# A convolution, Fourier and quantised feed-forward block: a new order of steps, the first image loaded ahead of the constants, and clearing on GpSimd

## The chip, the cores and the metric

The kernel runs on one core of a Trainium2 chip. The metric is the device time of one execution in microseconds (us). Before the change the median of three runs is 7464.09 us (7460.79 to 7466.0).

A core has engines with instruction queues of their own: TensorE (PE in the profile; its weight loads are PEld), VectorE (DVE), ScalarE (ACT), GpSimd (POOL) and SyncE (SP), which here only issues DMA transfers. Each queue is worked off in order, and the queues meet at semaphores.

## The reference, cut to what matters

For 64 images of 96 channels and 56x56 pixels:

```python
# layer 0
y = silu(bn(einsum('bchw,oc->bohw', x, expand_w)))       # 96 -> 192 channels
y = channel_shuffle(shift_groups(y))                     # four groups moved by one pixel
y = silu(bn(bn(depthwise3x3(y)) + bn(y * id_w)))
se = sigmoid(grouped(relu(grouped(mean(y, (2, 3))))))
x = silu(bn(einsum('bchw,oc->bohw', y * se, proj_w)) + x)
# layer 1, on t[b, n, c], n = 3136 pixels
h = relu(bn(layernorm(t) @ w1.T))
X = fft(h, axis=1); xr = relu(X.real*rd - X.imag*idg + rb); xi = relu(X.imag*rd + X.real*idg + ib)
t = t + bn(ifft(xr + 1j*xi, axis=1).real @ w2.T)
t = t + qlinear(relu(qlinear(layernorm(t), W1, b1)), W2, b2)   # operands rounded to 8 bits, sums to 16
```

## The kernel before, in words

The work on one image is cut into 56 kinds of step, and each kind has several instances: `x_in` 7 (eight image rows each), `ea_mm` 7, `i1_mm` 3, `h_mm` 21, `o_st` 7 and so on. A step is a small function (lines 376 to 912). Names that end in `_mm` issue matrix products on PE. `_ev` and its kin take a product out of PSUM, mostly on ACT (`ea_ev`, `dw_ev`, `h_ev`, `f1_ev`, `f2_u`, `i1_ev`) or on DVE (`w1_ev`, `i2_ev`, `f2_s`). `c_pow`, `n_pow` and `o_f` run on GpSimd. `x_in` and `o_st` issue two DMAs each on SP, which move an eighth-of-an-image stripe of the input or output.

The first layer of an image is `ea`/`eb` (expansion, the shift being a shifted window), `dw` (depthwise taps on PE for 128 channels) beside `lt` (nine taps on DVE for the other 64), `se` and `pj` (projection and residual). The second is `c`/`sp` (statistics), `w1`, the 56x56 Fourier transform in two factors (`f1`, `f2`), `w2`, the inverse in two factors (`i1`, `i2`), the second normalisation (`n`, `x`) and the feed-forward part (`h`, `o`).

Which step follows which is written out by hand. `PLAN` (lines 42 to 112) gives each instance a due time within an image, `PERIOD` the distance of two images; all instances of all images are sorted by due time and issued in that order (lines 921 to 928). The due times have no other use: they set the order within each queue, and by it also which buffer an instance gets, because a tile is handed out when it is issued and takes a buffer whose last reader has been issued.

```python
    with tc.manual_schedule():
        for _, b, k, i in sorted((b * PERIOD + when, b, k, i) for b in ... for k, step in ... for i, when in ...):
            STEPS[k](b, i)
```

Three images are in work at a time. There are two PSUM buffers of two banks (`psa_buf`, used by `w1`, `f1`, `f2`, `w2`, `i1`, `i2` in turn through `mix_ps`, line 356) and four of one bank (`psb`) for all else. There is one buffer `xi` for the padded input (line 166), so a stripe of the next image may be loaded once `pj_add` has read the rows that it overwrites.

Ahead of that list comes the setup (lines 166 to 354): loads of weights and tables on SP, ACT and GpSimd queues, folding of the normalisations into scales and shifts (`bn_fold`, `row_fold`), and clearing of buffers. Here the framework orders the instructions of each queue itself, and the order differs from that of the text. `row_fold` (line 260) fetches four rows of parameters to all partitions with a GpSimd DMA into a tile of two buffers (tag `ue`), takes a square root on ACT and works up the scale on DVE. It is called for the expansion, the projection, `bn1` (line 293, whose scale goes into `w1s`, line 298) and `bn2` in this order. The one product of the setup is L300, the centred `w1`; it stands first in PE's queue. The expansion's folded shift is copied into a row of `ex_w` by a DMA (line 277).

Of the kernel before, what the change touches and what calls it, by code (L numbers as in the profile page):

```python
# [7 lines left out]
F32 = mybir.dt.float32  # L8
F16 = mybir.dt.float16
F8 = mybir.dt.float8e5  # L10
AF = mybir.ActivationFunctionType
ALU = mybir.AluOpType
# [4 lines left out]
HW = 56  # L17
NPIX = HW * HW
MID = 192
HID = 384  # L20
CP = 112
TILES = ((0, 64), (64, CP))
GAP = 48
RPC = 8
NCH = HW // RPC
NT = 3
CH = RPC * HW
PAD = HW + 2
HH = HW // 2
PJ = 7  # L30
NG = 5
NK = HW // 2 + 1
NJ = HW // 2
# [8 lines left out]
PERIOD = 116.056  # L42
PLAN = {
    "x_in": (-142.751, -132.334, -138.890, -139.641, -151.208, -133.652, -137.370),
    "ea_mm": (-127.116, -124.446, -119.920, -94.498, -104.745, -112.167, -106.964),
    "ea_ev": (-125.252, -124.279, -119.721, -94.105, -94.974, -110.456, -105.960),
    "eb_mm": (-110.852, -109.364, -102.468, -94.672, -100.705),
    "eb_ev": (-109.889, -108.508, -98.175, -94.671, -100.704),
    "dw_mm": (-77.186, -75.415, -71.686, -59.708, -58.836, -58.630),
    "dw_ev": (-67.184, -68.088, -65.354, -62.005, -53.949, -53.481, -53.376, -53.432),  # L50
    "lt": (-93.236, -91.843, -90.397, -86.333, -83.176, -78.618, -75.060, -71.072, -58.358),
    "ls": (-56.957,),
    "se1_mm": (-52.674,),
    "se1_ev": (-52.590,),
    "se2_mm": (-49.560,),
    "se2_ev": (-47.764,),
    "se2_th": (-46.882,),
    "se2_pw": (-44.842,),
    "pj_mm": (-44.604, -44.263, -36.259, -33.499),
    "pj_add": (-41.623, -41.337, -40.573, -40.255, -32.468, -30.814, -32.509, -32.127),  # L60
    "pj_ev": (-41.036, -40.637, -40.429, -36.736, -30.334, -29.230, -31.146, -29.797),
    "c_mm": (-24.403, -20.404, -19.123, -17.297, -18.726, -9.644, -8.872),
    "c_sq": (-23.198, -19.663, -17.391, -16.366, -11.963, -8.651, -8.871),
    "c_v": (-21.831, -17.939, -17.390, -11.021, -10.842, -8.366, -8.657),
    "c_pow": (-19.058, -12.292, -10.931, -8.952, -1.526, -3.948, -1.526),
    "sp_v": (-8.951, -1.525),
    "sp_mm": (-6.057, 0.802),
    "sp_ev": (-5.461, 1.113),
    "w1_mm": (1.423, -2.619, 3.588, 18.203, 8.943, 12.171, 13.999, 16.535),
    "w1_ev": (3.273, -0.045, 7.600, 20.920, 11.591, 14.999, 15.957, 19.212),  # L70
    "f1_mm": (21.608, 26.248, 24.638, 31.810, 32.559, 32.004),
    "f1_ev": (25.169, 25.895, 30.841, 28.844, 27.556, 26.595, 32.009, 32.411, 36.910, 36.732, 36.699, 35.929),
    "f2_mm": (37.220, 36.994, 44.528, 54.196, 60.721, 63.959),
    "f2_u": (39.991, 41.910, 38.664, 38.665, 56.185, 56.316, 56.071, 58.643, 62.858, 62.962, 66.464, 67.055),
    "f2_s": (42.369, 43.646, 41.684, 42.524, 58.496, 59.412, 59.011, 59.603, 66.349, 66.780, 67.365, 69.133),
    "f2_r": (44.699, 46.227, 59.499, 60.966, 71.228, 72.985),
    "f2_p": (46.153, 47.154, 60.124, 60.967, 72.402, 74.345),
    "w2_mm": (70.359, 71.061, 73.352, 79.154),
    "w2_ev": (70.421, 73.788, 79.483, 82.773),
    "i1_mm": (82.811, 83.639, 91.924),  # L80
    "i1_ev": (86.931, 93.317, 99.344),
    "i2_mm": (102.107, 101.737, 110.644, 111.766),
    "i2_ev": (106.004, 107.037, 104.651, 104.395, 113.248, 110.645, 115.503, 113.393),
    "n_mm": (109.042, 108.523, 116.336, 120.505, 126.604, 126.539, 137.374),
    "n_sq": (109.105, 109.021, 116.337, 120.506, 127.174, 126.540, 137.375),
    "n_v": (109.642, 109.022, 116.338, 120.507, 127.975, 126.902, 138.122),
    "n_pow": (110.809, 110.170, 116.496, 122.658, 132.126, 129.135, 139.318),
    "n_x": (112.520, 110.693, 119.248, 123.053, 133.298, 130.929, 139.362),
    "x_mm": (113.125, 114.113, 121.321, 126.216, 135.244, 138.382, 142.002),
    "x_ev": (114.896, 115.709, 126.025, 126.217, 137.926, 142.365, 142.302),  # L90
    "h_mm": (
        144.408, 144.539, 142.955, 151.653, 146.123, 151.741, 165.593, 167.081, 167.021, 179.037, 181.701, 184.163,
        183.315, 191.401, 194.122, 202.572, 203.025, 214.978, 205.482, 214.132, 209.133,
    ),
    "h_ev": (
        146.457, 147.163, 146.728, 153.132, 153.156, 154.262, 168.465, 171.753, 169.119, 180.037, 185.733, 184.280,
        187.040, 192.972, 195.243, 203.531, 205.107, 216.376, 208.878, 222.205, 212.052,
    ),
    "h_b": (
        146.899, 148.834, 148.614, 154.505, 157.941, 159.836, 170.515, 176.287, 174.097, 185.812, 187.639, 185.918,  # L100
        191.781, 195.030, 198.861, 204.123, 206.545, 220.428, 209.152, 226.370, 218.475,
    ),
    "h_q": (
        149.384, 151.139, 150.029, 159.215, 163.340, 163.159, 172.257, 183.329, 182.397, 187.024, 188.763, 189.403,
        196.328, 198.478, 200.406, 208.755, 210.002, 221.499, 217.314, 229.791, 224.579,
    ),
    "o_mm": (153.028, 179.101, 192.712, 203.850, 207.474, 223.800, 230.382),
    "o_ev": (154.015, 179.621, 193.552, 207.958, 209.955, 223.824, 232.254),
    "o_b": (167.276, 193.254, 201.506, 209.696, 210.604, 235.187, 237.499),
    "o_f": (171.766, 199.519, 206.356, 219.602, 231.322, 259.139, 253.186),  # L110
    "o_st": (197.792, 218.616, 214.282, 229.895, 257.122, 313.688, 263.438),
# [4 lines left out]
def conv_attn_ffn(  # L116
# [38 lines left out]
    nc = tc.nc  # L155
    NB = x.shape[0]

    const = ctx.enter_context(tc.tile_pool(name="const", bufs=1))
# [10 lines left out]
    nc.sync.dma_start(out=xi[GAP : GAP + 1].rearrange("p a b -> p (a b)"), in_=tab_ones)  # L169

    def load_x(b, i):

        rows = slice(i * RPC, (i + 1) * RPC)
        for p0, c0 in ((0, 0), (64, 48)):
            nc.sync.dma_start(
                out=xi[p0 : p0 + 48, 1 + i * RPC : 1 + (i + 1) * RPC, 1 : HW + 1],
                in_=x[b, c0 : c0 + 48, :].rearrange("c (a b) -> c a b", b=HW)[:, rows, :],
            )


    def load(ap, shape, name, eng=nc.sync, dtype=F32):
        t = const.tile(shape, dtype, name=name)
        eng.dma_start(out=t, in_=ap)
        return t

    ex_w = load(expand_t, [CP, MID], "ex_w")
    mid = load(mid_par, [128, 2, 22], "mid")
    mid_g = load(mid_grp, [128, NG, 12], "mid_g")
# [19 lines left out]
    l_tab = load(tab_l, [128, NK, CP], "l_tab", nc.scalar)  # L208
    inv_tab = load(tab_inv, [CP, 2, HW], "inv_tab", nc.scalar)
    r_tab = load(tab_r, [128, HW, HW], "r_tab", nc.scalar)  # L210

    eps = const.tile([128, 1], F32, name="eps")
    nc.vector.memset(eps, 1e-5)
    mhalf = const.tile([128, NJ], F32, name="mhalf")
    nc.vector.memset(mhalf, -0.5)
# [35 lines left out]
    eyes = load(tab_eyes, [128, 32], "eyes")  # L251
# [7 lines left out]

    def row_fold(src, n, rows, name):  # L260

        b = work.tile([128, 4, n], F32, tag="ue", name=name + "_p")
        nc.gpsimd.dma_start(out=b[0:rows], in_=src.rearrange("(o f) c -> o f c", o=1).to_broadcast([rows, 4, n]))
        s = work.tile([128, 2, n], F32, tag="s", name=name)
        s = s[0:rows]
        nc.scalar.activation(s[:, 0], b[0:rows, 3, :], AF.Sqrt, bias=eps[0:rows])
        nc.vector.reciprocal(s[:, 0], s[:, 0])
        nc.vector.tensor_tensor(s[:, 0], s[:, 0], b[0:rows, 0, :], ALU.mult)
        nc.vector.tensor_tensor(s[:, 1], b[0:rows, 2, :], s[:, 0], ALU.mult)
        nc.vector.tensor_tensor(s[:, 1], b[0:rows, 1, :], s[:, 1], ALU.subtract)  # L270
        return s

    s = row_fold(expand_row, MID, CP, "ex_row")
    nc.vector.tensor_tensor(ex_w, ex_w, s[:, 0], ALU.mult)
    nc.sync.dma_start(out=ex_w[GAP : GAP + 1, :], in_=s[0:1, 1, :])
    ex_b = const.tile([CP, 2, 2, 2, 16], F32, name="ex_b")
    nc.vector.memset(ex_b, 0.0)
    for e in range(2):  # L280
        nc.vector.tensor_copy(
            ex_b[:, e, :, e, :], ex_w[:, 128:MID].rearrange("p (u e i) -> p u e i", u=2, e=2)[:, :, e, :]
        )
# [43 lines left out]

    e_a = const.tile([128, PAD, PAD], F32, name="e_a")  # L330
    nc.gpsimd.memset(e_a, 0.0)
    e_b = const.tile([128, HH + 2, PAD], F32, name="e_b")
    nc.gpsimd.memset(e_b, 0.0)
    for i in range(NT):
        nc.vector.memset(t_buf[i], 0.0)

    buf_h = const.tile([128, C * HW + 8], F32, name="buf_h")
    nc.vector.memset(buf_h, 0.0)
# [6 lines left out]
    nc.vector.memset(buf_g, 0.0)  # L345
# [30 lines left out]
    def x_in(b, i):  # L376
        load_x(b, i)
# [726 lines left out]
```

## Time and profile before

| | |
|---|---|
| median of three runs | 7464.09 us |
| the profiled execution: its time | 7463.64 us |
| its span, first to last instruction | 7461.9 us |
| PE / PEld / DVE / ACT / POOL busy | 7176.9 / 5259.2 / 4829.5 / 4654.4 / 1513.6 us |
| PE idle in all | 285.0 us |
| first matrix product (L300) | at 43.30 us |
| last matrix product | 7453.65 us |
| PE busy from 300 to 7300 us | 6822.69 of 7000 us |

A wait in the profile is the idle time of an engine just before an instruction, put down to what released it. "issue" means that nothing which the profile records was waited for. Lines such as L786 are lines of the kernel before; `psa`, `ps_c` and so on are the tiles that are written.

PE's order in one period, from the sort (the number in brackets is the image, relative to the one whose `dw` it starts with; adjacent instances of one kind are put together):

```
before
dw0 dw1 dw2[0] f2_2[-1] h6 h8 h7[-2] f2_3[-1] dw3 dw4 dw5[0] f2_4[-1] h9[-2] o1[-2] se1[0] f2_5[-1] h10[-2] se2[0]
h12 h11[-2] w2_0 w2_1[-1] pj0 pj1[0] w2_2[-1] h13 o2 h14[-2] w2_3[-1] pj2 pj3[0] i1_0 i1_1[-1] h15 h16 o3 h18 o4[-2]
c0[0] i1_2[-1] h20[-2] c1 c2 c4[0] h19[-2] c3[0] h17[-2] i2_1 i2_0[-1] ea0[1] c5 c6[0] ea1[1] o5[-2] n1 n0[-1] sp0[0] ...
after
dw0 dw1 dw2[0] f2_2[-1] h6 h8[-2] f2_3[-1] dw3 dw4 dw5[0] f2_4[-1] h7[-2] f2_5[-1] h9[-2] o1[-2] se1[0] h10 h12 h11[-2]
se2[0] w2_0 w2_1[-1] pj0 pj1[0] w2_2[-1] h13 h14 o2[-2] w2_3[-1] pj2 pj3[0] i1_0[-1] o3 h16 h15[-2] i1_1[-1] o4 h18[-2]
i1_2[-1] h20[-2] c0 c1 c2 c4[0] h19 h17[-2] i2_0 i2_1[-1] ea0[1] c3 c5 c6[0] ea1[1] o5[-2] n1[-1] sp0[0] n0[-1] ...
```

ACT's order around the second half of `dw`: before `dw_ev4 dw_ev5 dw_ev7 dw_ev6 f2_u8 f2_u9 se1_ev`, after `dw_ev7 dw_ev6 f2_u8 h_ev7 f2_u9 dw_ev5 dw_ev4 h_ev9 o_ev1 se1_ev`. SP's order from the projection on: before `x_in4, o_st, o_st, x_in0` amid the `pj_add`, then `x_in3 x_in2 x_in6 o_st x_in5 x_in1 o_st`; after `x_in0` amid the `pj_add`, one `o_st`, and behind the last `pj_add` `x_in6 x_in2 x_in1 x_in5 x_in4 o_st o_st x_in3`.

### The profile page before, as it was taken

To read this page: it belongs to the slowest core of one execution; us is meant where nothing else is said; L and a number is where in the kernel's file an instruction comes from. 1 tells how busy PE (TensorE), PEld (TensorE's weight loads), DVE (VectorE), ACT (ScalarE), POOL (GpSimd) and SP (SyncE) were. 2 spreads that over 40 slices of the span, in tenths; PEclk is the share of its full clock that TensorE was granted. 3 is DMA by queue.
4 is the path that set the end of the run, shared out by engine and by line. 5 is a ranking of instruction groups with operands and counts; after the bars stand their busy time and mean duration, and the time that the engine had idled before them with its cause. 6 is when DMAs were issued, how large, how long until landed. Compare 5 with 4: busy or idle time off the path is not lost.

```text
span 7461.9 us, 383252 instructions
## 1 busy us (share of the span) xinstructions
PE 7176.9 (96%) x177666; PEld 5259.2 (70%) x177666; DVE 4829.5 (65%) x8795; ACT 4654.4 (62%) x9806; POOL 1513.6 (20%) x1360
## 2 busy tenths in 40 slices
PE   7999999999999999999999999999999999999997
PEld 4777777777777776777777777777777777777775
DVE  5666666666666666666666666666666666666664
ACT  3566666666665666656656666666566566665665
POOL 0221212212212122122121221221212212212112
PEclk9999999999999999999999999999999999999998
DMA  1010110110101101101011011010110110101100
GB/s 48 20 27 18 29 27 19 29 24 21 28 17 29 27 19 28 24 22 28 17 29 27 19 28 25 22 28 18 29 27 19 29 26 20 29 21 26 28 20 21
DMA packets 424331, 185.32 MB, mean 25 GB/s; under 512 B 378785, under 2 KB 422041, under 8 KB 422473
## 3 DMA queue, kind: packets, MB, share of 16 engines
q1 hardware_dynamic: 420970, 155.82, 9.1%
q8 instruction: 1392, 22.81, 1.3%
q10 hardware_dynamic: 1264, 3.48, 0.1%
q14 instruction: 209, 1.71, 0.1%
q0 software_dynamic: 496, 1.50, 0.1%
HBM read 82.80 MB, written 77.07 MB: 21 GB/s over the span
## 4 chain that ended last, share of the span: by engine, by line
PE 85%; ACT 6%; DVE 6%; issue 3%; DMA 0%; POOL 0%; POOLq 0%; SPq 0%; ACTq 0%
PE psa L653 9%; PE psa L626 9%; PE ps_d L446 8%; PE ps_eb L400 5%; PE ps_ea L383 5%; PE psa L808 5%; PE ps_pj L532 5%; PE ps_c L557 5%; PE psa L745 5%; PE ps_n L557 5%; PE psa L786 5%; PE psa L680 4%; PE ps_h L865 4%; PE ps_o L887 3%; DVE s L721 3%
## 5 line engine op out<-in xcount | busy, mean ns | idle before, releaser
L903 POOL TENSOR_TENSOR o<-t,o 112x448 f32<-112x448 f32 x448 | 613.9, 1370 | 3694.7 <-DMA out_dram<-o 1710.0
L446 PE MATMUL ps_d<-e_a,diag 32*32 32x392 f32 x36864 | 1033.2, 498 | 0.7 <-ACT d L456 0.7
L468 DVE SCALAR_TENSOR_TENSOR d_last<-e_b,taps,d_last 128x1568 f32<-128x1568 f32 x512 | 971.5, 1898 | 7.1
L875 DVE TENSOR_SCALAR y<-y,qb 128x448 f16<-128x448 f16 x1344 | 479.8, 365 | 683.9 <-ACT y L870 676.7
L568 DVE TENSOR_REDUCE v<-sq 112x4 f32<-112x384 f32 x896 | 491.3, 548 | 662.7 <-ACT sq L564 662.1
L446 PEld LDWEIGHTS ps_d<-e_a,diag 32*32 32x32 f32 x36864 | 673.6, 103 | 288.9 <-issue 40.0
L870 ACT CAST y<-ps_h 128x448 f16<-128x448 f32 x1344 | 697.2, 540 | 213.1 <-PE ps_h L865 209.5
L837 POOL TENSOR_TENSOR rs<-v,mhalf 112x4 f32<-112x4 f32 x448 | 490.3, 1099 | 1453.9 <-DVE v L569 1453.9
L881 ACT CAST h<-y 128x448 fp8e5<-128x448 f16 x1344 | 739.0, 571 | 3.0 <-DVE y L875 3.0
L653 PEld LDWEIGHTS psa<-f_tab,buf_h 128*56 128x56 f32 x24576 | 655.4, 131 | 77.8 <-DVE v L569 42.5
L626 PEld LDWEIGHTS psa<-w1c,t 112*64 112x64 f32 x14336 | 604.0, 137 | 141.4 <-DVE v L569 45.4
L653 PE MATMUL psa<-f_tab,buf_h 128*56 128x58 f32 x24576 | 688.9, 216 | 0.0
L626 PE MATMUL psa<-w1c,t 112*64 112x96 f32 x14336 | 676.2, 249 | 2.9 <-DMA t<-dev_t 1.4
L586 POOL TENSOR_TENSOR rs<-v,mhalf 112x4 f32<-112x4 f32 x448 | 447.6, 1012 | 763.6 <-DVE v L569 763.5
L638 DVE SCALAR_TENSOR_TENSOR buf_h<-psa,rs_full 128x768 f32<-128x768 f32 (+1 forms) x512 | 435.4, 851 | 137.4 <-PE psa L626 129.5
L543 DVE TENSOR_TENSOR ps_pj<-ps_pj,x 112x392 f32<-112x392 f32 x512 | 260.6, 566 | 404.5 <-PE ps_pj L537 392.3
L728 ACT ACTIVATE s<-s 128x896 f32<-128x896 f32 (+2 forms) x384 | 334.4, 887 | 288.8 <-DVE s L721 288.8
L388 ACT ACTIVATE e_a<-ps_ea 128x448 f32<-128x448 f32 x448 | 244.9, 547 | 412.5 <-PE ps_ea L383 412.5
L564 ACT ACTIVATE sq<-ps_n 112x384 f32<-112x384 f32 x448 | 214.1, 495 | 436.1 <-PE ps_n L557 434.8
L734 DVE SCALAR_TENSOR_TENSOR buf_h<-ue,s 128x448 f32<-128x448 f32 (+2 forms) x768 | 406.8, 580 | 109.4 <-ACT s L728 109.4
L549 ACT ACTIVATE t<-ps_pj,pjbn_b 112x392 f32<-112x392 f32 x512 | 281.4, 620 | 284.5 <-DVE ps_pj L543 284.5
L786 PE MATMUL psa<-inv_tab,buf_g 112*32 112x56 f32 x24576 | 350.5, 214 | 110.5 <-issue 108.8
(175 smaller groups left out, 13024.5 us busy)
## 6 DMA issues: line engine op xcount, KB each, us to landing
x<-in_x SPq DMA_DIRECT2D x896, 84.0 KB, 3.2
out_dram<-o SPq DMA_DIRECT2D x896, 84.0 KB, 2.2
l_tab<-in_tab_l ACTq DMA_DIRECT2D x1, 1624.0 KB
r_tab<-in_tab_r ACTq DMA_DIRECT2D x1, 1568.0 KB
t<-dev_t SPq DMA_DIRECT2D x64, 7.0 KB, 2.1
t<-dev_t SPq DMA_DIRECT2D x64, 5.2 KB
ex_row_p<-in_expand_row POOLq DMA_DIRECT2D x1, 336.0 KB, 4.5
s_p<-in_bn POOLq DMA_DIRECT2D x1, 288.0 KB, 3.8
```

What stands on the lines that cost most here:

```text
L446: nc.tensor.matmul(pss[r][j * 32 : j * 32 + 32], lhsT=diag[pr, tap, :], rhs=e_a[pr, r0 : r0 + PJ, dx : dx + HW], start=tap == 0, stop=tap ...
L468: nc.vector.scalar_tensor_tensor(d_last, win, w, d_last, ALU.mult, ALU.add)
L557: nc.tensor.matmul(cen[c0:c1, k, 0:C], lhsT=t_of(b)[:, n0 + c0 : n0 + c1], rhs=center, start=True, stop=True)
L568: nc.vector.tensor_reduce(v, sq, AX.X, ALU.add)
L626: nc.tensor.matmul(ps[hc * 64 : hc * 64 + 64, k, 0:C], lhsT=t[:, n0 : n0 + 64], rhs=w1c[:, hc * C : hc * C + C], start=True, stop=True,)
L653: nc.tensor.matmul(ps[r * 64 : r * 64 + HW, k, 0 : 2 * NK], lhsT=buf_h[:, n0 : n0 + HW], rhs=f_tab[:, r, :], start=True, stop=True,)
L786: nc.tensor.matmul(ps[p0 : p0 + 32, k, 0:HW], lhsT=u_v[:, oh * 48 + o, :], rhs=inv_tab[:, r, :], start=True, stop=True,)
L837: nc.gpsimd.tensor_tensor(rs, held.pop(("nv", b, g)), mhalf[0:CP, 0:4], ALU.pow)
L870: nc.scalar.copy(y16, held.pop(("h", b, i)))
L875: nc.vector.tensor_scalar(y16, y16, qb1[:, i % 3 : i % 3 + 1], 0.0, ALU.add, ALU.max)
L881: nc.scalar.copy(held["h8", b, j][:, m, :], held.pop(("y", b, i)), saturate=False)
L903: nc.gpsimd.tensor_tensor(o32, rows, o16, ALU.add)
```

## The change

It has three parts.

1. `PERIOD` and all due times of `PLAN` are replaced. The kinds of step, their number and what each does stay as they are; the order in every queue is new.
2. In the setup the load of the expansion weights is followed at once by the row of ones, the 14 DMAs of the first image (taken out of the sorted list by `if b > 0`) and the fold of the expansion with its `ex_b`. `mid`, `mid_g` and `eyes` go to ACT's queue; the two big tables `l_tab` (1624 KB) and `r_tab` (1568 KB) leave ACT's queue and come last of the loads, on SP. The copy of the folded shift goes from SP to GpSimd.
3. The clearing of the three `t_buf`, `buf_h` and `buf_g` goes from DVE to GpSimd, and that of `e_a` and `e_b`, on GpSimd already, moves up in the text.

The diff, with the rows of the plan that the prediction speaks of:

```diff
-PERIOD = 116.056
+PERIOD = 116.1319138
...
-    "x_in": (-142.751, -132.334, -138.890, -139.641, -151.208, -133.652, -137.370),
+    "x_in": (-152.0645309, -141.2993712, -141.6679729, -127.3567477, -140.4175705, -140.8791946, -144.4420607),
...
-    "dw_ev": (-67.184, -68.088, -65.354, -62.005, -53.949, -53.481, -53.376, -53.432),
+    "dw_ev": (-77.0167479, -77.0167407, -77.0167341, -77.0167381, -60.0783737, -60.0901315, -61.6632225, -61.9014126),
...
-    "i1_mm": (82.811, 83.639, 91.924),
+    "i1_mm": (80.9444124, 84.7640673, 88.5170591),
...
-    "o_mm": (153.028, 179.101, 192.712, 203.850, 207.474, 223.800, 230.382),
+    "o_mm": (144.4008021, 172.4113645, 192.8051961, 197.2106880, 201.6982825, 222.7674293, 226.6091401),
...
     nc.vector.memset(xi, 0.0)
-    nc.sync.dma_start(out=xi[GAP : GAP + 1].rearrange("p a b -> p (a b)"), in_=tab_ones)
...
     ex_w = load(expand_t, [CP, MID], "ex_w")
-    mid = load(mid_par, [128, 2, 22], "mid")
-    mid_g = load(mid_grp, [128, NG, 12], "mid_g")
+
+    nc.sync.dma_start(out=xi[GAP : GAP + 1].rearrange("p a b -> p (a b)"), in_=tab_ones)
+    for i in range(NCH):
+        load_x(0, i)
+    eps = const.tile([128, 1], F32, name="eps")
+    nc.vector.memset(eps, 1e-5)
...
+    s = row_fold(expand_row, MID, CP, "ex_row")
+    nc.vector.tensor_tensor(ex_w, ex_w, s[:, 0], ALU.mult)
+    nc.gpsimd.dma_start(out=ex_w[GAP : GAP + 1, :], in_=s[0:1, 1, :])
...
+    e_a = const.tile([128, PAD, PAD], F32, name="e_a")
+    nc.gpsimd.memset(e_a, 0.0)
+    e_b = const.tile([128, HH + 2, PAD], F32, name="e_b")
+    nc.gpsimd.memset(e_b, 0.0)
+
+    mid = load(mid_par, [128, 2, 22], "mid", nc.scalar)
+    mid_g = load(mid_grp, [128, NG, 12], "mid_g", nc.scalar)
+    eyes = load(tab_eyes, [128, 32], "eyes", nc.scalar)
...
-    l_tab = load(tab_l, [128, NK, CP], "l_tab", nc.scalar)
     inv_tab = load(tab_inv, [CP, 2, HW], "inv_tab", nc.scalar)
-    r_tab = load(tab_r, [128, HW, HW], "r_tab", nc.scalar)
...
-    nc.sync.dma_start(out=ex_w[GAP : GAP + 1, :], in_=s[0:1, 1, :])
...
+    l_tab = load(tab_l, [128, NK, CP], "l_tab")
+    r_tab = load(tab_r, [128, HW, HW], "r_tab")
...
     for i in range(NT):
-        nc.vector.memset(t_buf[i], 0.0)
+        nc.gpsimd.memset(t_buf[i], 0.0)
...
-    nc.vector.memset(buf_h, 0.0)
+    nc.gpsimd.memset(buf_h, 0.0)
...
-    nc.vector.memset(buf_g, 0.0)
+    nc.gpsimd.memset(buf_g, 0.0)
...
     def x_in(b, i):
-        load_x(b, i)
+        if b > 0:
+            load_x(b, i)
```

## The prediction

> **What bounds the kernel now.** The page comes first. PE is busy for nearly the whole span and no other engine comes near it:
>
> ```profile
> PE 7176.9 (96%) x177666; PEld 5259.2 (70%) x177666; DVE 4829.5 (65%) x8795; ACT 4654.4 (62%) x9806; POOL 1513.6 (20%) x1360
> ...
> PE   7999999999999999999999999999999999999997
> ```
>
> The change takes no matrix product away. What it can gain lies in PE's 285.0 us of idle time (7461.9 - 7176.9), of which 43.3 us come before the first product. So the second view is the waits, asked for PE alone, with sum, number and longest:
>
> ```profile
> PE psa L786 <- issue: 108.8, 68, 2.2
> PE psa L745 <- DVE ue L724: 50.8, 64, 1.7
> PE ps_w1c L300 <- DVE w1s L298: 43.3, 1, 43.3
> PE ps_c L557 <- issue: 18.6, 20, 1.9
> ```
>
> Two waits come in every one of the 64 images: about 1.7 us in `i1_mm` (L786) for nothing recorded, and 0.8 us in `w2_mm` (L745) for `f2_s`. With the 18.6 us in `c_mm`, "issue" costs 127.4/64 = 2.0 us an image. The third view is PE's timeline of one image amid the run, to see where these fall:
>
> ```profile
> 3028.02 0.61 PE L478 MATMUL ps_se<-sums,rd_w 128*24 128x1 f32 x18
> ...
> 3031.92 1.53 PE L745 MATMUL psa<-w2a,buf_h 128*64 128x96 f32 x32 [0.83 <-DVE ue L724]
> ...
> 3050.09 2.86 PE L786 MATMUL psa<-inv_tab,buf_g 112*32 112x56 f32 x216
> 3055.03 1.00 PE L786 MATMUL psa<-inv_tab,buf_g 112*32 112x56 f32 x40 [2.08 <-issue]
> ...
> 3059.89 1.78 PE L786 MATMUL psa<-inv_tab,buf_g 112*32 112x56 f32 x128
> ```
>
> The third `i1_mm`, standing alone, runs its 128 products (and 128 loads) in 1.78 us without a break; the first two, standing together, stop after 216 of 256. No semaphore does that. The page's queue table names a suspect:
>
> ```profile
> q8 instruction: 1392, 22.81, 1.3%
> ```
>
> 22.81 MB in 1392 packets is 16.4 KB a packet, and 2 x 177666 instructions over 1392 packets is 255 a packet: PE's instructions arrive in blocks of about 256. One `i1_mm` uses up a block in 1.7 us, faster than any other step (`dw`: 576 instructions in 7.95 us). I read the wait as the next block being late: a block needs about 1.7 + 1.75 = 3.5 us to come. SP's timeline shows the six DMAs of `x_in` starting at 3050.79, so these blocks travel beside image data.
>
> [...] I go with the row, which recurs in each image where two `i1_mm` adjoin and not where one stands alone.
>
> **Steady part, step by step.**
> (a) *`i1`.* The new order puts `o3 h16 h15` between the first two (rows: 0.66 + 0.55 = 1.2 us) and `o4 h18` (0.67 + 0.28 = 0.95 us) before the third. Every block of 256 in this stretch (3 x 256 + 18 instructions) now holds one such gap: 1.7 + 1.2 = 2.9 us or 1.7 + 0.95 = 2.65 us instead of 1.7. Against 3.5 us two boundaries wait 0.6 and 0.85, and a third, half in `c_mm`, perhaps 0.1: 1.55 instead of 2.0. Besides, `x_in6` and its followers now start only behind the last `pj_add`, some 2.1 us into the stretch (the four take 1.99 us), so the first block may come sooner. I take -0.5 us an image. Ends: -1.4 (every block but one in time), and +1.2, if the unbroken run of `x_in` makes a block take 4.1 us: then the two wait 1.2 and 1.45 and the third 0.5, 3.2 in all.
> (b) *`w2`.* From the start of `f2_4` to that of `w2_0` the old order takes 3031.92 - 3025.66 = 6.26 us, 0.83 of it waiting. In the new one `h7` (0.2 us) moves in here, and `se1` comes to lean on `dw_ev4`, now last: from the start of `f2_4`, ACT does `dw_ev7`, `dw_ev6` (to 1.3), waits for `f2_4` (1.56), then `f2_u8`, `h_ev7`, `f2_u9` (0.6 + 0.45 + 0.6) and `dw_ev5`, `dw_ev4` (2 x 0.565), to 4.4 us. PE arrives at 1.5 + 0.3 + 1.1 + 0.3 + 0.66 = 3.85 and waits 0.6. With `se1`, three `h` and `se2` (0.54 + 0.67 + 0.65) `w2_0` starts at 6.3, and its `f2_s9` (3.25 + 4 x 0.65 = 5.85) is done: this wait goes, the one at `se1` comes. Behind `se1` stand the `h` products and `se2`, whose followers `se2_pw` and `pj0` have over 1 us to spare. Net 0; ends -0.3 and +0.4.
> (c) *The rest of the period.* I walked the queues in the same way. The spare times are small but not negative: `pj0` for `h_ev12` 0.35 us, `x0` for `n_x0` 0.45, `f1_4` for `f1_ev2` 0.6, `f2_1` for `f1_ev11` 0.3. Adjoining `h` products fall into 11 groups instead of 13, worth 0.1 each at most. Zero; ends -0.2 and +0.3.
> Sum: -0.5 us an image, over 63 images -32 us.
>
> **Start.** Here PE is held by L300, first in its queue:
>
> ```profile
> 4.07 2.92 POOL L331 MEMSET e_a<- 128x3364 f32 x1
> ...
> 22.49 4.54 DVE L338 MEMSET buf_h<- 128x5384 f32 x1 [1.06 <-issue]
> ...
> 33.33 0.53 POOL L263 DMA_DIRECT2D s_p<-in_bn  x1 [10.98 <-DVE ex_row L270]
> ...
> 43.30 0.98 PE L300 MATMUL ps_w1c<-w1s,gcen 96*112 96x192 f32 x2 [43.30 <-DVE w1s L298]
> ```
>
> The parameters of `bn1` are fetched at 33.33 because their buffer waits for the expansion's fold (L270), which sits in DVE behind three memsets of 2.68, one of 4.54 and loads of later constants. With the fold early and these memsets gone, its parameters (landing 4.5 us after 1.28) give a square root by about 7 and L270 by about 10. Fetch, square root and scale then take 3.87 + 0.46 + 1.34 + 3 x 0.35 = 6.7 us, so L300 could start at 17.3 and `ea` 0.9 later, at 18.2 instead of 44.20: 26 us gained. But the memsets, and now the shift's copy too, share GpSimd's queue with this fetch. At the rate of the `e_a` row (2.92/3364 = 0.87 ns a column) they take 3 x 2.73 + 4.67 + 4.83 = 17.7 us; all ahead of the fetch, behind `e_b` (8.5), it goes out at 26.8, and `ea` starts at 34.5: 9.7 us gained. Which it is depends on how the framework sorts the setup; I take the middle, -18 us. The cover for the memsets is that `t_buf` is first written at 88 us and `buf_h` at 111.
>
> The 14 DMAs of `x` (11 took 8.56 us to issue) go out from the end of the `xi` memset (4.4) and are done by some 17 us; if SP serves the two tables first (3.2 MB; the first 20 us ran at 271 GB/s, so 12 us), they end near 29, still within the span above. `mid`, `mid_g` and `eyes` add three issues of 0.45 us to ACT's queue, ahead of the square roots; the two tables that leave it gave back 0.8. `diag`, which needs `mid` and some 30 small DVE operations (26.96 to 31.96 now), is wanted 12.8 us after `ea`, when `dw` begins; DVE, free of 17.3 us of memsets, has that time. `l_tab` is needed at 141 us and `r_tab` at 200. Uncovered, a late `diag` would hold `dw` for what it is late; I put nothing.
>
> **The end.** The last 55 us (7407 to 7462) are a chain of normalisation and feed-forward steps of one image; its order changes little: 0, +-4.
>
> Sum against the profiled execution: 7463.64 - 32 - 18 = 7413.6, and the median of the runs is 0.45 above it: 7414 us.
>
> **Rivals.**
> (B) *The fetch of blocks gains nothing* (three dense blocks near each other wait as long as two did), and only the start moves: 7464 - 18 = 7446, between 7437 and 7455. For it: the stretch still holds 768 instructions in some 8 us. Against it: no two `i1_mm` adjoin.
> (C) *Slower: the blocks meet the transfers.* Place: the boundaries in `i1_1` and `i1_2`. Five stripes of `x_in` and two of `o_st` now follow each other without a break there. At 4.1 us a block the price is 3.2 - 2.0 = 1.2 us an image, 7464 + 76 - 18 = 7522. It decides from 0.52 us an image on ((18 + 15)/63), that is from about 3.75 us a block. For it: the longest wait before is 2.2 us, 3.9 a block. Against it: that was under the old burst, which began earlier.
> (D) *More than thought*: blocks in time but one and an early start: 7464 - 63 x 1.4 - 26 = 7350.
>
> **How the numbers follow.** Forecast (A) 0.55, own range 7385 to 7448; B 0.22; C 0.13; D 0.10. A measurement of this kernel can tell about 0.2% (15 us) from no change: below 7449 is faster, above 7479 slower. A lies below with 0.54, D with 0.10, B with 0.13 of its 0.22: 0.77 faster. C is 0.13 slower. 0.10 is left for the same. The range takes A, B, half of D and the beginning of C: 7368 to 7475.
>
> **What would show it.** Right: `ea` (L383) starts between 18 and 34 us; L786 shows several short waits on "issue" an image, under 1.6 us together, none of 2; L745's wait on L724 is gone and L478 waits for L456 instead. Wrong: the sum of waits on "issue" at or above 127 us (B, C); a new wait in each image on DVE, ACT or POOL that (c) has not; PE busy time off 7177 by more than 20 us.

## The result, and the profile after

The kernel after the change takes 7414.07 us (median of four runs, 7406.62 to 7424.39), the kernel before beside it 7464.03 us: a ratio of 0.9939 [0.9925, 0.9953], 50 us faster. The profiled execution has a span of 7414.7 us, 47.2 below that of before. Measured again later beside other kernels it took 7423.54 against 7467.66 us, 0.9946 [0.9932, 0.9959], 44 us. So two sets of the same comparison differ by 6 us, and smaller differences are read from traces here, not from medians.

Line numbers have moved: L809 is `i1` (it was L786), L580 `c` and `n` (L557), L768 `w2` (L745), L501 `se1` (L478), L747 `f2_s` (L724), L479 `dw_ev` (L456), L324 the first product (L300), L406 `ea` (L383). First the engine line of the page after:

```profile
PE 7188.3 (97%) x177666; PEld 5229.7 (71%) x177666; DVE 4842.3 (65%) x8790; ACT 4641.4 (63%) x9806; POOL 1589.9 (21%) x1366
```

PE's idle time is 7414.7 - 7188.3 = 226.4 us, 58.6 less than before; its busy time is 11.4 us longer. The waits of PE, after (sum, number, longest):

```profile
PE psa L809 <- issue: 97.5, 112, 2.0
PE ps_w1c L324 <- DVE w1s L322: 26.2, 1, 26.2
PE ps_c L580 <- issue: 24.5, 23, 2.9
PE ps_se L501 <- ACT d L479: 16.4, 65, 1.3
...
PE psa L768 <- DVE ue L747: 1.6, 2, 1.4
```

Three things are to be seen. The wait ahead of `w2` is gone (50.8 to 1.6 us) and one at `se1` has come (16.4). The first product starts 17.1 us earlier. But the waits on "issue" have hardly moved: 108.8 + 18.6 = 127.4 before, 122.0 now. PE's timeline of one `i1` stretch after shows why:

```profile
3031.22 1.78 PE L809 MATMUL psa<-inv_tab,buf_g 112*32 112x56 f32 x128
3032.93 0.77 PE L910 MATMUL ps_o<-h,q 128*112 128x448 fp8e5 x3
3033.54 0.54 PE L888 MATMUL ps_h<-xq,q 96*128 96x448 fp8e5 x2
3034.01 1.39 PE L809 MATMUL psa<-inv_tab,buf_g 112*32 112x56 f32 x96
3035.75 0.60 PE L809 MATMUL psa<-inv_tab,buf_g 112*32 112x56 f32 x32 [0.35 <-issue]
3036.28 0.78 PE L910 MATMUL ps_o<-h,q 128*112 128x448 fp8e5 x3
3036.89 0.35 PE L888 MATMUL ps_h<-xq,q 96*128 96x448 fp8e5 x1
3037.18 1.37 PE L809 MATMUL psa<-inv_tab,buf_g 112*32 112x56 f32 x92
3039.79 0.69 PE L809 MATMUL psa<-inv_tab,buf_g 112*32 112x56 f32 x36 [1.23 <-issue]
```

The one long pause of 2.08 us has become two shorter ones. Counted through the whole trace, every distance of over 0.7 us between two neighbouring starts of one line's loads and products (83 before, 94 after, between 300 and 7200 us) falls at the same remainder of PE's instruction count divided by 256: they are block boundaries, as the prediction read them. Summed over all boundaries between 300 and 7200 us, what these distances have beyond the usual cost 149.5 us before and 145.6 after, 0.06 us an image less.

The spans add up as follows. `dw` of the first image starts 17.3 us earlier (56.98 to 39.69). From there to `dw` of the fourth image the new order takes 6.6 us longer (311.4 to 318.0). After the `dw` of the last image it takes 4.2 less (209.7 to 205.5 us to the last product). What is left of the 47.2, some 32 us, is the period, which falls from 114.65 to 114.07 us (mean over images 3 to 60).

### The profile page after: what moved, and what is told of

Same layout as the page of the kernel before. It is cut to its first block, busy times and chain, and to the rows that moved or that the text cites. A ratio compares the mean times of both kernels' runs of the same rounds, so it can differ in the third digit from the quotient of the medians.

```text
span 7414.7 us, 383547 instructions
## 1 busy us (share of the span) xinstructions
PE 7188.3 (97%) x177666; PEld 5229.7 (71%) x177666; DVE 4842.3 (65%) x8790; ACT 4641.4 (63%) x9806; POOL 1589.9 (21%) x1366
## 4 chain that ended last, share of the span: by engine, by line
PE 93%; ACT 3%; issue 3%; DVE 1%; POOL 0%; DMA 0%; POOLq 0%; ACTq 0%; SPq 0%
PE ps_d L469 14%; PE psa L676 9%; PE psa L649 9%; PE ps_ea L406 5%; PE ps_eb L423 5%; PE psa L831 5%; PE ps_n L580 5%; PE ps_pj L555 5%; PE psa L768 5%; PE psa L809 4%; PE ps_c L580 4%; PE psa L703 4%; PE ps_h L888 4%; PE ps_o L910 3%; PE psa L713 3%
## 5 line engine op out<-in xcount | busy, mean ns | idle before, releaser
L926 POOL TENSOR_TENSOR o<-t,o 112x448 f32<-112x448 f32 x448 | 659.1, 1471 | 3629.9 <-DVE o L920 2280.0
L688 ACT COPY buf_g<-psa 128x464 f32<-128x464 f32 x768 | 388.8, 551 | 186.4 <-PE psa L676 184.7
L809 PE MATMUL psa<-inv_tab,buf_g 112*32 112x56 f32 x24576 | 373.3, 214 | 99.3 <-issue 97.5
L809 PEld LDWEIGHTS psa<-inv_tab,buf_g 112*32 112x32 f32 x24576 | 327.5, 110 | 197.5 <-issue 196.3
L866 DVE TENSOR_TENSOR xt<-ps_n,rs 112x384 fp8e5<-112x384 f32 x448 | 243.7, 556 | 315.8 <-POOL rs L860 311.4
```

Source lines behind the costliest of these rows:

```text
L809: nc.tensor.matmul(ps[p0 : p0 + 32, k, 0:HW], lhsT=u_v[:, oh * 48 + o, :], rhs=inv_tab[:, r, :], start=True, stop=True,)
L926: nc.gpsimd.tensor_tensor(o32, rows, o16, ALU.add)
```

## The experiments

**The two halves of the change.** `setup_only` has the new setup with the old plan, `plan_only` the new plan with the old setup (both keep everything else).

> The new setup with the old period and due times. If the parts simply add: the first matrix product at about 26 us instead of 43.3, and all of these 17 us kept to the end, 7447. If the new order is what loses 6.9 us of the start in the first two images (first dw to fourth dw: 311.9 us before, 318.9 after), this run keeps 311.9 and ends at 7447; if the new setup itself loses them (a table or a buffer that comes late), it shows 319 and ends at 7454.

> The new period and due times with the old setup; the first image is then loaded from the setup's queue position as before. If the parts add: first product at 43.3 us, and 7464 minus 30, 7434. The prediction's steady term alone would give 7432. If the gain of the new order needs the new start, it ends near 7464.

Measured: `setup_only` 7445.21 us, 0.9979 [0.9972, 0.9986]; `plan_only` 7438.44 us, 0.9966 [0.9958, 0.9974]; before 7463.55. The parts give 18.3 + 25.1 = 43.4 us, the whole 44 to 50: they add, within the 6 us by which two sets differ. The first product starts at 26.2 us in the one and at 43.2 in the other. The 6.6 us lost in the first images belong to the new order: from the first `dw` to the second `setup_only` needs 87.05 us, as before (87.10), `plan_only` 92.6, as after (92.4). The period is 114.66 with the old plan and 114.14 with the new.

**Step (a) undone.** `i1_together` puts the first two `i1_mm` back to back:

```diff
-    "i1_mm": (80.9444124, 84.7640673, 88.5170591),
+    "i1_mm": (80.9444124, 80.9454124, 88.5170591),
```

> The changed kernel with one due time moved, so that the second i1_mm follows the first at once and o3 h16 h15 come behind it. The prediction's step (a): two blocks in a row again, 0.5 us an image more waiting, 7414 + 32 = 7446. The rival (blocks under the unbroken run of x_in take about 4 us, so that splitting and not splitting wait alike, as the sums of the two traces say: 149.5 us before, 145.6 after): 7414, within 10 us, with waits of 2 us again in i1_mm and fewer of them.

Measured: 7421.45 us, 0.9953 [0.9937, 0.9968], and these waits:

```profile
PE psa L809 <- issue: 105.4, 102, 2.2
...
PE ps_c L580 <- issue: 22.6, 24, 2.9
```

128.0 us instead of 122.0 (118.4 in the second trace of after). The parting of the `i1_mm` is worth some 6 to 10 us of waits in all, not 32, and the time is where the rival had it. Step (a) falls.

**Do the blocks meet the image transfers?** `no_x` leaves out the loads of images 1 to 63, seven stripes each (`NB` is the number of images, 64):

```diff
-        if b > 0:
+        if b > NB:
             load_x(b, i)
```

> after without the loads of the image stripes of images 1 to 63: all images are computed from the pixels of the first, as they stand in the buffer; everything else is as in after. Theory that PE's instruction blocks are late because they travel beside the image transfers: the waits on issue in i1 and c (97.5 + 24.5 us) fall below 60 us, and the time by as much, to about 7350. Rival that a block takes 3.0 us and more whoever else transfers: the waits stay at 105 us or more and the time within 20 us of 7414.

Measured: 7395.02 us in one run, and

```profile
PE psa L809 <- issue: 82.7, 111, 1.7
...
PE ps_c L580 <- issue: 20.2, 22, 2.9
```

102.9 us, 19 less than after, and the time of this one run is 19 us less too. So the meeting that rival (C) was built on exists, but it makes about one sixth of the waits; the rest comes whether images are loaded or not. Neither expectation had the figure; the second was nearly right.

**Step (b), and where the clock comes in.** In the waits of after, `se1` waits for `dw_ev4`. `dw_ev5_early` puts ACT's `f2_u9` and `dw_ev5` further forward, to take that wait away:

```diff
-    "dw_ev": (..., -60.0783737, -60.0901315, -61.6632225, -61.9014126),
+    "dw_ev": (..., -60.0783737, -61.6500000, -61.6632225, -61.9014126),
...
-        56.0332668, 59.7855946, 59.8827469,
+        54.8412044, 59.7855946, 59.8827469,
```

> The changed kernel with dw_ev5 put ahead of f2_u8 and f2_u9 ahead of h_ev7 on ScalarE. By the walk of step (b): se1 can start 0.4 us earlier (dw_ev4 is done at 4.05 instead of 4.4 us behind the start of f2_4), and w2_0 is still not held by f2_s9: 0.4 us an image less, 7414 - 25 = 7389. If the wait only moves on to w2_0 or se2, no change.

Measured: 7457.24 us (median of twelve, 7445.96 to 7465.32; the profiled one is the longest), 0.9996 [0.9987, 1.0004], 43 us slower than after. The wait at `se1` did go; a smaller one at `w2` came back:

```profile
PE psa L768 <- DVE ue L747: 28.3, 65, 1.6
...
PE psa L768 <- DVE gate L529: 5.9, 37, 0.2
```

28.3 + 5.9 - 16.4 - 1.6 = 16 us of waits do not make 43. PE's timeline of that kernel shows the rest:

```profile
3135.15 0.76 PE L501 MATMUL ps_se<-sums,rd_w 128*24 128x1 f32 x18
3135.84 0.86 PE L888 MATMUL ps_h<-xq,q 96*128 96x448 fp8e5 x3
3136.63 0.43 PE L516 MATMUL ps_se<-red,ep_w 24*32 24x1 f32 x32
3136.99 0.28 PE L524 MATMUL ps_se<-red,ep_w 24*64 24x1 f32 x4
3137.68 2.65 PE L768 MATMUL psa<-w2a,buf_h 128*64 128x96 f32 x32 [0.42 <-DVE ue L747]
```

The 32 products of `w2` take 2.65 us, where they take 1.53 in other images. The same kernel asked by stretches (start:end, length, busy us and count of PE, PEld, DVE, ACT and POOL, granted TensorE clock, DMA share, GB/s):

```profile
3131.10:3134.50 3.40, 3.40 (x62) 2.56 (x52) 1.68 (x4) 3.00 (x9) 0.00 (x0) 1.00 0.02 5
3134.50:3137.90 3.40, 2.98 (x66) 1.81 (x66) 2.93 (x7) 3.40 (x10) 0.00 (x0) 1.00 0.00 0
3137.90:3141.30 3.40, 3.40 (x60) 3.18 (x60) 3.05 (x8) 2.66 (x7) 1.31 (x1) 0.50 0.00 0
3141.30:3144.70 3.40, 3.40 (x92) 2.77 (x88) 1.69 (x5) 2.42 (x6) 0.00 (x0) 1.00 0.02 5
```

For one stretch of 3.41 us PE is granted half its clock. The trace notes each change of the clock: such stretches begin only at multiples of 3.413 us from one another, within 0.01 us over the whole run (all 24 in the trace of before and all 16 in that of after as well), so they are windows of a grid. In the window before this one PE waits 0.42 us and issues products of one column (L501, L516, L524) for another 1.3. The kernel before has the same thing elsewhere. Its stretches around the 2.08 us pause that the prediction showed:

```profile
3048.50:3051.90 3.40, 3.40 (x159) 2.45 (x159) 1.71 (x4) 1.10 (x3) 0.00 (x0) 1.00 0.07 15
3051.90:3055.30 3.40, 1.32 (x108) 1.20 (x100) 0.52 (x2) 1.79 (x4) 1.31 (x1) 0.99 0.64 130
3055.30:3058.70 3.40, 3.40 (x43) 2.03 (x32) 0.67 (x2) 1.56 (x4) 0.00 (x0) 0.50 0.58 131
```

Busy for 1.32 of 3.40 us, and the next window runs at half speed. Between 300 and 7200 us these windows sum to 54.6 us before, 23.9 after and 102.4 in `dw_ev5_early`; half of the 78.5 us between the last two is 39 us, and with the 16 us of waits that is 55, against 43 between the medians and 49 between the two profiled spans. In `dw_ev5_early` they come at 3137.9, 3254.0, 3370.0 and 3486.1 us: 116.05 us apart, which is 34 windows (34 x 3.413). An image that is hit becomes so long that the next one meets the grid at the same place.

**Taking the wait away.** DVE stood idle for 2.12 us ahead of `f2_s8`, held by `h_b7`, which waited for ACT. `h7_late` is `dw_ev5_early` with `h_b7` behind `f2_s9`:

```diff
-        ..., 152.3035773, 164.4059572, 171.8564611,
+        ..., 152.3035773, 164.4059572, 176.2000000,
```

> This is dw_ev5_early with one more due time moved: the DVE half of h7 (h_b7, 171.86 to 176.2) goes behind f2_s9 instead of ahead of f2_s8, where DVE stood idle for 2.12 us waiting for ACT's h_ev7. w2_0 should then find f2_s9 done. Clock theory (a PE window of 3.41 us with 1.6 us or more of idle and single-column products is followed by one at half speed; in dw_ev5_early the 0.42 us wait at w2 brings the stretch se1 to w2 to 1.75 us): without the wait the stretch has 1.35, the half-speed windows at w2 vanish (25 in dw_ev5_early, 3 in after), and the time falls by the wait and by half of some 85 us of half-speed windows: 7457 - 28 - 42 = 7387, between 7380 and 7400, faster than after by 15 to 30. Rival (the loss of dw_ev5_early is the wait at w2 and what comes after it, the clock has no part): 7457 - 28 = 7429, between 7420 and 7440. Second rival (the wait moves to another place): within 7414 to 7460, with a new wait of 0.3 us or more in each image.

Measured: 7402.33 us (7399.5 to 7410.45), 0.9917 [0.9901, 0.9934]. Half-speed windows fall from 102.4 to 10.2 us between 300 and 7200 us, and none is left at `w2`, where `dw_ev5_early` had 25. The time falls by 55 us where the waits at `w2` fell by 19 (28.3 + 5.9 to 13.6 + 1.8): the clock theory's side, 2 us outside its range. Half of the 92 us of half-speed windows and the 19 us of waits make 65, against 62 between the two profiled spans. The miss has a name in this kernel's timeline:

```profile
3119.29 0.63 DVE L744 SCALAR_TENSOR_TENSOR s<-psa,fb,ue 128x392 f32<-128x392 f32 x1 [1.70 <-ACT ue L728]
...
3124.36 0.15 DVE L529 TENSOR_TENSOR gate<-ps_se,ep_b 128x5 f32<-128x5 f32 x1
3124.59 1.53 PE L768 MATMUL psa<-w2a,buf_h 128*64 128x96 f32 x32 [0.22 <-DVE gate L529]
```

`f2_s8` now waits only for its own operand, but the second `w2` waits 0.22 us in 62 images (13.6 us) for DVE, which does `h_b9` and `o_b1` ahead of `f2_s10`. `h9_late` moves these behind the gate as well:

```diff
     "h_b": (
...
-        162.0938148, 176.2691390, 188.9411972, ...
+        162.0938148, 181.6000000, 188.9411972, ...
...
     "h_q": (
...
-        168.8971320, 181.6666748, 191.8993395, ...
+        168.8971320, 182.6000000, 191.8993395, ...
...
-    "o_b": (158.1581711, 179.3239824,
+    "o_b": (158.1581711, 181.6100000,
```

> This is h7_late with three more steps moved behind what the projection waits for: h_b9 and o_b1 on DVE from ahead of f2_s10 to behind se2_ev, h_q9 on ACT behind se2_th. In h7_late, w2_1 waited 0.22 us in 62 images (13.6 us) for DVE, which had done these two first (0.33 us each). Theory that the wait simply goes: 7402 - 13 = 7389, between 7383 and 7396, with no wait at w2 left. Rival that PE finds another wait in its place (h_q9 later on ACT, o2 later): 7398 to 7406, with a new wait of about 0.2 us in each image.

> The kernel after the change, unaltered, beside h9_late and clear_dve. By its runs so far: 7407 to 7424, median 7414; with half-speed PE windows from 300 to 7200 us of 15 to 45 us in all, as many as the time is longer by half of them.

Measured side by side: `h9_late` 7386.23 us (7382.75 to 7390.35), 0.9891 [0.9878, 0.9905]; after 7423.54 us (7421.79 to 7432.35), 0.9946 [0.9932, 0.9959]. The waits at `w2` are gone and no new one came. `h9_late` beats both kernels: 81 us below before and 37 below after. Of the 37, 64 x 0.36 = 23 lie between the last `dw` product and `w2` (6.60 us an image after, 6.23 here; 13 of them are the recorded waits at `se1`, 16.4 to 3.0), and the clock gives (118.9 - 91.1)/2 = 14, counted over the whole run. The two profiled executions of after differ in the same way, with nothing changed: spans of 7414.7 and 7420.0 us, half-speed windows of 23.9 and 34.1 us between 300 and 7200 us. Half of the difference is 5.1, the spans differ by 5.3.

**Is it single-column work, and not only idling, that lowers the clock?** `se1_twice` and its control `h_twice` issue products of `h9_late` a second time:

```diff
 se1_twice, in se1_mm
-        for i in range(9):
+        for _ in range(2):
+            for i in range(9):
 h_twice, in h_mm
-        nc.tensor.matmul(ps, ...)
+        for _ in range(2 if i in (10, 12) else 1):
+            nc.tensor.matmul(ps, ...)
```

> This is h9_late with the 18 products of se1 issued twice (the second pass overwrites the first with the same sums): 0.69 us more of single-column products an image, and no wait. Clock theory (single-column products count as idle for the clock, and a 3.41 us window with some 1.6 us of both is followed by one at half speed): from the first se1 product to w2 the stretch is then 2.75 us long and has 2.02 us of single-column work; of the positions of a fixed window 1.5/3.41 = 0.44 catch 1.6 us or more of it, so at least 28 of 64 images have a half-speed window at w2, at about 1.5 us each: 7386 + 44 + 42 = 7472 and up to 7526 if all images have one. Rival (only waits count, not single-column products, since PE is busy): 7386 + 44 = 7430, between 7424 and 7438, and no half-speed window at w2.

> The control of se1_twice: h9_late with the products h10 and h12, which stand between se1 and se2, issued twice (same result): two more products of 448 columns, 0.57 us an image, in the same place. Both theories: 7386 + 36 = 7422, between 7414 and 7430, and no half-speed window at w2, since nothing sparse is added. If half-speed windows come here too, it is the longer distance from dense work to dense work and not the single columns that counts.

Measured: `se1_twice` 7417.33 us, 0.9920 [0.9904, 0.9937]; `h_twice` 7395.97 us, 0.9894 [0.9879, 0.9909]. Both sizes were wrong: the second pass costs 0.33 us an image, not 0.69 (from `se1` to `w2` 2.06 to 2.39 us), since the row of 0.76 us contained a wait between products (in the trace of after they start 0.025 to 0.046 us apart and once 0.37 us, 0.21 of it recorded as idle); the two `h` cost 0.26, not 0.57. Both times lie below the ranges of both theories, and so do not decide between them. The sparse work of that stretch rose to some 1.7 us only, not 2.02. The direction holds, though at least 28 half-speed windows were expected: at `w2` there are 5 with `se1_twice` and none in `h9_late` or `h_twice`; in all, 30.7 us against 13.7 and 3.4. Stretches of `se1_twice` around one of the five:

```profile
2778.90:2782.30 3.40, 3.40 (x85) 2.35 (x85) 2.72 (x6) 3.31 (x10) 0.00 (x0) 1.00 0.00 0
2782.30:2785.70 3.40, 3.40 (x56) 3.18 (x58) 3.33 (x9) 2.84 (x7) 0.76 (x1) 0.51 0.02 5
```

PE counts as busy for all of the first stretch, and the second runs at half speed. So recorded idle time is not needed. But a row of `se1` contains a short wait that in part counts as busy: whether the single columns or this wait lower the clock, the two runs cannot tell. Five windows are few; the control has none. Against `h9_late` the profiled span is 33.7 us longer (7417.5 to 7383.8): 64 x 0.33 = 21 and, over the whole run, half of 118.0 - 91.1, 13.

**The start.** `clear_only` is before with the five memsets on GpSimd; `clear_dve` is after with them back on DVE.

> before with the clearing of the three t_buf, of buf_h and of buf_g on GpSimd, and nothing else. Theory that the memsets on DVE are what holds the expansion's fold (L270) and so bn1's fetch: the first product starts at 26 to 32 instead of 43.3 us. Rival that the clearing only changes the queue in which it stands ahead of the fetch (GpSimd issues it): the first product starts at 38 us or later. Time: 7464 less what the first product gains, to within 6 us.

> after with the clearing of the three t_buf, of buf_h and of buf_g back on DVE: part 3 undone, the new order of the setup kept. Theory that the loads and the fold in their new place bring the early start and the clearing has little part: the first product starts at 20 to 28 us (26.2 in after). Rival that DVE's 17 us of clearing holds the fold again: the first product starts at 34 us or later. Time: 7414 and what the first product moves, to within 8 us.

`clear_only`: first product at 42.9 us, 7474.4 us in one run against 7465.45 (9 us longer where at most 6 were expected, but inside the scatter of before, whose runs went from 7443 to 7479). Part 3 alone brings nothing; the rival holds. `clear_dve`: first product at 22.0 us, 4.2 earlier than after, and yet 7435.25 us in one run, 12 more than after beside it, where 4 less was expected. Its timeline:

```profile
6.51 0.17 DVE L260 TENSOR_SCALAR fa<-fa 128x2 f32<-128x2 f32 x1 [1.95 <-DMA fa<-in_freq_a]
...
13.33 0.52 POOL L216 DMA_DIRECT2D s_p<-in_bn  x1
...
14.28 0.29 DVE L291 TENSOR_SCALAR taps<-mid,dwbn_s,mgbn_s 128x9 f32<-128x9 f32 x1
...
38.91 4.70 DVE L367 MEMSET buf_g<- 128x5568 f32 x1 [1.11 <-issue]
...
64.19 0.48 PE L501 MATMUL ps_se<-sums,rd_w 128*24 128x1 f32 x8 [8.30 <-ACT d L479]
```

and that of after:

```profile
6.04 5.15 DVE L260 TENSOR_SCALAR fa<-fa 128x2 f32<-128x2 f32 x1 [1.48 <-DMA fa<-in_freq_a]
...
8.43 2.74 POOL L357 MEMSET t<- 112x3144 f32 x1
...
16.34 0.51 POOL L230 DMA_DIRECT2D ex_w<-ex_row  x1 [5.17 <-DVE dwbn_b L275]
...
16.88 0.52 POOL L216 DMA_DIRECT2D s_p<-in_bn  x1
...
17.39 2.74 POOL L357 MEMSET t<- 112x3144 f32 x1
...
17.87 2.29 DVE L291 TENSOR_SCALAR taps<-mid,dwbn_s,mgbn_s 128x9 f32<-128x9 f32 x1
...
26.19 0.98 PE L324 MATMUL ps_w1c<-w1s,gcen 96*112 96x192 f32 x2 [26.19 <-DVE w1s L322]
27.10 4.93 PE L406 MATMUL ps_ea<-x,ex_w 112*32 112x448 f32 x32
```

A scaling of two columns takes 0.17 us in the one and 5.15 in the other, where it ends (11.19) as GpSimd's memset ends (11.17). The scaling of `taps`, 0.29 us there, takes 2.29 here and ends at 20.16, as the next memset ends (20.13). In both pairs of rows DVE's instruction ends within 0.03 us of GpSimd's memset; what the two share was not shown, nor why the first scaling, from 6.04 us on, did not slip in before 8.43, when GpSimd issued DMAs. Behind it the fold is late, GpSimd's copy of the folded shift waits for DVE until 16.34, and the fetch of `bn1` behind that goes out at 16.88 instead of 13.33, 3.5 us later. What the clearing on GpSimd buys comes afterwards: with it on DVE, the taps of the first image start behind the memset of `buf_g`, and `se1` waits 8.30 us.

## Why the prediction came out where it did

The time was predicted to 0.1 us, and that closeness is luck: two sets of the same comparison differ by 6 us, and the steady part and the start each came near their figure by terms that the sum did not have. The signs named for "right" could not tell this either. `ea` started at 27.10 us, the wait at `w2` went and one at `se1` came, the waits in `i1` were 97.5/64 = 1.5 us an image and PE's busy time was off by 11.4 us, all as said but for one wait of 2.0 us, although the gain in `i1` did not come.

**Start: -18 predicted, 17.1 measured at the first product, and 10.7 kept.** The fetch went out at 16.88 us, between the bounds that were worked out from GpSimd's queue. Only one of the memsets that moved to GpSimd stood ahead of it there, but beside this one DVE's scaling took 5.15 us instead of 0.17, which the step did not have. What the sum left out is the filling: the new order takes 6.6 us longer over the first three images, 5.3 of it from the first `dw` to the second. There PE runs the same number of products of each kind, is busy 81.1 us instead of 77.3 and idle 11.4 instead of 9.8; five half-speed windows instead of three lie in that stretch (17 us against 10), and half of the difference, 3.4 us, is most of the busy time's 3.8.

**Step (a), `i1`: -0.5 us an image predicted, -0.06 measured.** This is the step that failed. It counted what a block of 256 instructions contains and held the time of its arrival at 3.5 us for every block. A first late boundary does come 3.5 us after the boundary before it (median of 67 in the trace of after, between 300 and 7200 us, with distances of over 0.4 us taken as late). But a second one in a row comes 4.0 us after the first (median of 69); the timeline above has 2.80 us of work and 1.23 of waiting between the two. With 4.0 the sum of step (a) has waits of 0.6, 1.35 and 0.1, and nothing is gained on 2.0: the same waits came in smaller portions. 4.0 us is near rival (C)'s time, but not for its reason: without the image loads the second still takes 3.7 (median of 64 in `no_x`). Why a second block takes longer than a first is open. PE's recorded idle time on "issue" between 300 and 7200 us did fall more, from 123.9 to 110.9 us. Yet where no half-speed window falls, the stretch from the first `i1` to the first `i2` is as long as before: 14.0 us less 0.8 for a `c` that has left it, against 13.2. That the waits are those of blocks was right, and they do cost PE time, as said: 122.0/64 = 1.9 us an image.

**What stood in its place: the clock.** From the first `i1` to the first `i2`, 16 of 58 images before have a half-speed window and take 15.48 us, the other 42 take 14.00; after, it is 4 images (14.60) and 54 (13.24, without that `c`). That is 0.41 us an image before and 0.09 after: -0.31. At `w2` three images after have one, +0.08. The counts vary with the execution: the second trace of after has 2 such images at `i1` and 8 at `w2`, `plan_only` 2 and 11; with the old order `setup_only` has 18 and `clear_only` 19 at `i1`, none at `w2`. So the gain at `i1` belongs to the new order. That the breaking up of the long pause brought it is not shown, and `i1_together` speaks against it: with the two `i1_mm` adjoining again it has 5 such images, not 16. The longest pause of an image in this stretch has a median of 1.64 us before, 1.22 after and 1.50 in `i1_together`; which moves of the new order shortened it there is open.

**Step (b), `w2`: 0 predicted (-0.3 to +0.4), -0.28 measured.** From the first `dw` to the first `w2`, where PE has the same products in both orders, 26.20 us became 25.92. The wait at `w2` went as said; the one at `se1` is 0.25 us, not 0.6. These two recorded waits fell by more, 50.8 - 1.6 - 16.4 = 32.8 us or 0.5 an image; what took the rest back was not looked for.

**Step (c), the rest: 0 predicted, about 0 measured.** -0.06 - 0.31 + 0.08 - 0.28 = -0.57, which is what the period fell by in this pair of traces. Within it the stretch from `f1` to `dw` gained some 0.3 (adjoining `f1` and `x` products) and others gave it back. **The end** gave 4.2 us, just outside its +-4; its cause was not looked for.

So rival (B) was right about the fetch and wrong about the time, because it held that nothing else would move. The sum, -32 in the steady part and -18 at the start, met -32, -10.7 and -4.2. Of the measured -32 some 18 us are step (b) and some 15 the clock.

## What to carry to other kernels

A pause of PE can cost twice: once as a wait, and again as half speed in the next window, which no list of waits shows (`dw_ev5_early`, against after: 16 us more of waits, 78.5 us more of half-speed windows). Ask for the granted clock in stretches around each pause and each run of one-column products, not only its mean. In a queue that is ordered by hand, look for instructions that need an operand late and stand ahead of one that PE waits for: six due times moved with this in view took 37 us off the kernel after, 14 of them by the clock, while the whole new order of steps alone had taken off 25. The first two of the six alone cost 43 us: they brought one short wait (0.42 us) to a place with 1.3 us of one-column products.

## What the runs showed of the hardware that was not expected

- Half-speed windows follow windows that are not idle. The longest of PE's recorded pauses between 300 and 7200 us is 2.19 us before and 2.01 after, in windows of 3.41 us, and yet 16 and 7 half-speed windows (54.6 and 23.9 us) fall there. In all fourteen traces each of them follows a window with about 1.45 us or more of idle time and one-column products together (1.56 and more before, 1.46 and more after); every window with more than 1.9 us was followed by one, and those between went either way. Recorded idle time alone does not sort them: some followed windows with 0.3 us of it or less (three with 0.29 after), and none followed others with up to 1.88 (before). So in these traces the border lies between 1.45 and 1.9 us of 3.41; exactly where, and what is counted, they do not tell.
- In `dw_ev5_early` the loss locked in: with images of 34 windows (116.05 us), 25 of 58 lost 1.35 us each (19.74 instead of 18.39 us from the first `w2` to the first `i1`).
- At a block boundary amid the run the next load or product of PE started up to 2.4 us behind the one before it (before), and 19 of 122 us of these waits come from image loads (`no_x` against after, one run). A second late block in a row takes 4.0 us, the first 3.5 (medians, after). What sets the rest was not tried.
- A DVE instruction of 0.17 us (`clear_dve`) took 5.15 beside a GpSimd memset (after), and one of 0.29 us took 2.29.
